# A four-layer graph network: row sums as two short-float parts, and a product moved ahead of its layer

## The chip, the cores and the metric

The kernel runs on one core of one Trainium2 chip, in one launch. The metric is the device time of one execution in microseconds. The engines are named as in the profile: PE (TensorE matmuls), PEld (its weight loads), DVE (VectorE), ACT (ScalarE), POOL (GpSimd) and SP (SyncE, which here issues most plain DMAs).

## The reference

There are N = 4096 nodes with 512 features and E = 65536 edges, sorted by destination. Each of four layers normalises the rows, applies a relu, runs a layer on the graph and adds the result to x. The second and third, layers 1 and 2, are the ones to see:

```python
# each layer: h = max(layernorm(x), 0); x = x + layer(h)
# layer 1; row, col = src, dst with a loop of every node appended
agg = segment_sum(vals[:, None] * x[col], row)          # vals = deg^-1/2[row] * deg^-1/2[col]
return relu(agg @ weight)
# layer 2
edge_feat = concatenate([x[src], x[dst], edge_attr], -1)
h = mish(edge_feat @ W1 + b1)
messages = mish(h @ W2 + b2)
agg = segment_sum(messages, dst)
u = mish(concatenate([x, agg], -1) @ W3 + b3)
y = x + u @ W4 + b4
return (y - mean(y)) * rsqrt(var(y) + eps) * gamma + beta
```

Layer 0 is an attention over the edges with eight heads, and layer 3 is a graph convolution like layer 1. All of it is computed in fp32.

## The kernel before

Nodes are held in NB = 32 blocks of P = 128, one node per partition. Edges are held in W = 512 tiles of 128, and U = 4 tiles make a group, so that there are NG = 128 groups. D is 512, KC = D/P = 4. A large SBUF tile `acc` holds one row per node and is what segment sums add into.

**Layer 1** (`sum_edges`, L865 to L913, which layer 3 uses as well). The table of rows times W already lies in DRAM (`ytab`). For each tile, POOL issues an indirect DMA (`gather`, L424) which fetches the 128 rows that its edges name; this runs four groups ahead, into six buffers. ACT makes a one-hot matrix of the edges' places in a window of nodes (Abs at L871, Relu at L876), and PE multiplies it with the gathered rows (L903), in fp32. Eight tiles share one PSUM bank; DVE then adds the bank into at most two blocks of `acc` (`add_window`, L436). Which layer runs is told by `tail` and `per`; layer 1 has `tail=0` and `per=PAIR=2`.

**Between** (L952 to L1034). As soon as a block of 128 nodes has all its edges, its next steps are issued beside the sums of later blocks: relu (L973), the sum with x1 (L975; the result goes to `x2`), mean and variance (L361), the reciprocal root through Ln and Exp with one Newton step (L982 to L989), the normalised relu (L990, L991, stored as `h2`), four transposes (L996), their copy to SBUF (L998), and two products with the halves of W1 (L1003). These are stored as `ptab` and `qtab` (L1011), so that layer 2 only has to gather and add two rows for an edge. `block` is a Python generator: each `yield` is a place where the sums go on. `follow` is called after every second tile; it begins block b when 16(b+1)+8 tiles have been issued and eight calls have passed since the last, and it steps the blocks that are under way. `the_rest` issues what is left at the end. `by_destination` (L261) prepares the lists of edges by destination beside layer 1 in the same way.

**Layer 2, messages** (L1143 to L1205). Before it, `acc` is filled with zeros, one half by DVE (L1059) and one by ACT (L1060). Then, for each group: gathers from `ptab` (L424) and adding gathers from `qtab` (L1085), the part of W1 that meets the edges' attributes (L1102), mish, transposes (L1109), the product with W2 (L413), mish, and a sum by destination. This sum already uses two short-float parts: a value is rounded to the type fp32r (L1122), the rest is a second fp32r value (L1123), and two fp32r matmuls (L1129) take the place of one fp32 matmul.

**Layer 2, end** (`layer2_ends`, L1211 to L1347). Blocks are taken in pairs (R = 2), in 16 steps. A step transposes h2 and the sums (L1277, copied at L1279), makes u transposed (64 matmuls on 128x256, L1302, with b3 added at L1304), runs mish through Sigmoid, Arctan and Sin (L1306 to L1308), multiplies with W4 (L413), adds h2 (L1320), normalises (`Norm2`, L1246 to L1270, with a root by bit tricks and Newton steps), applies gamma and x2 (L1330, L1332), stores x3, normalises once more and writes the relu scaled by `dis` (L1344) to `ztab` for layer 3. POOL adds b4 to h2 (L1293) and beta to x2 (L1314).

**Layer 3** (`Ending`, L1351 to L1420) sums by destination with the same `sum_edges`, and runs the last product and the output of each block beside these sums.

The order of instructions on PE, ACT, DVE and POOL is the order in which the program writes them (`tc.manual_schedule`). An engine works its queue in order, so one that waits holds up what is queued behind it; SP's queue of DMA issues is in order too. The table below gives the main names once more.

| name | what it is |
|---|---|
| `g`, `got` | gathered rows of a group, and the groups under way |
| `oh` | one-hot matrices of a group |
| `sum_ps` | PSUM bank of eight tiles' sums |
| `side`, `follow` | work issued between the sums |
| `ptab`, `qtab` | DRAM tables of h2 times the two halves of W1 |
| `tr`, `h_t`, `a_t`, `u_t` | transposes, and what is copied of them |

Of the kernel before, what the change touches and what calls it, by code (L numbers as in the profile page):

```python
# [34 lines left out]
def kernel(  # L35
# [225 lines left out]
    def by_destination(pool, ppool):  # L261
# [5 lines left out]
        three = pool.tile([P, 3, W], F32, name="three_d")  # L267
        for j in range(2):
            nc.vector.tensor_copy(three[:, j, :], ends[:, j, :])
            yield  # L270
        loc_i = pool.tile([P, W], I32, name="loc_i")
        nc.vector.tensor_scalar(loc_i, ends[:, 1, :], P - 1, None, op0=OP.bitwise_and)
        nc.vector.tensor_copy(three[:, 2, :], loc_i)
        yield
        for k, into in enumerate((d_src, d_dst, d_loc)):
            ps = ppool.tile([P, 4, P], F32, name="turn")
            of = three[:, k, :].rearrange("p (q j) -> p j q", j=U)
            for j in range(U):
                nc.tensor.transpose(ps[:, j, :], of[:, j, :], ident)
            yield  # L280
            yield
            nc.vector.tensor_copy(into.rearrange("p (g j) -> p j g", j=U), ps)
            yield
        node = three[:, 1, :]
        rise = pool.tile([P, W], F32, name="rise")
# [13 lines left out]
        down = pool.tile([1, NG], F32, name="down")  # L299
# [565 lines left out]
    def sum_edges(table, idx, loc, bi, half, per, beside=None, follow=None, tail=0):  # L865

        def made_one_hots(pool, minus, t0):

            oh = pool.tile([P, U, P], F32, name="oh")
# [6 lines left out]
            nc.scalar.activation(oh, oh, AF.Relu, scale=-1.0, bias=1.0)  # L876
            return oh, short

        with tc.tile_pool(name="edge", bufs=3) as ep, tc.tile_pool(name="edge_ps", bufs=4, space=PSUM) as eps, \
# [3 lines left out]
            got, ohs = {}, {}  # L883
            side = Side(*(beside(bp, bps) if beside else ()))
            for i in range(-4, NG):
                if i + 4 < NG:
                    g = got[i + 4] = ep.tile([P, U, D + tail], F32, name="g", bufs=6)
                    for j in range(U):
                        t = (i + 4) * U + j
                        gather(g[:, j, :], table, idx[:, t:t + 1])  # L890
                if 0 <= i + 1 < NG:
                    ohs[i + 1] = made_one_hots(ep, loc, (i + 1) * U)
                if i < 0:
                    continue
                g, (oh, short) = got.pop(i), ohs.pop(i)
# [6 lines left out]
                for j in range(U):  # L902
                    nc.tensor.matmul(ps[:, :D], oh[:, j, :], g[:, j, :D], start=i % per == 0 and j == 0,  # L903
                                     stop=i % per == per - 1 and j == U - 1)
                    if tail and j % 2:
                        follow(i * U + j + 1)
                    if j == U - 1 and i % per == per - 1:
                        add_window(i // per, bi, half, wide_at if tail else row_at, ps[:, :D + 3] if tail else ps)
                    if j % 2 and not tail:
                        side.step()  # L910
                        if follow:
                            follow(i * U + j + 1)
# [38 lines left out]

    class Between:  # L952
# [4 lines left out]
        def __init__(self, pool, ppool):  # L957
            self.pool, self.ppool, self.next, self.xs, self.going, self.since = pool, ppool, 0, {}, [], self.APART
            for b in range(self.AHEAD):
                self.load(b)  # L960
            self.w1_sb = load_w(pool, "w1_sb", w1[:2 * D])
            self.b1_bc = row_bc(pool, "b1_bc", b1)

        def load(self, b):
            if b < NB:
                self.xs[b] = self.pool.tile([P, D], F32, name="x_mid", bufs=self.AHEAD + 2)
                nc.sync.dma_start(self.xs[b], x1[b * P:(b + 1) * P, :])

        def block(self, b):
# [9 lines left out]
            nc.vector.tensor_scalar(st[:, 1:], st[:, 1:], EPS, None, op0=OP.add)  # L979
            root = pool.tile([P, 1], F32, name="root_mid", bufs=2)  # L980
# [14 lines left out]
            for k in range(KC):  # L995
                nc.tensor.transpose(ps[:, k, :], hn[:, k * P:(k + 1) * P], ident)  # L996
            h_t = pool.tile([P, KC, P], F32, name="ht_mid", bufs=2)
            nc.scalar.copy(h_t, ps)  # L998
            yield
            for k0, tab in ((0, ptab), (KC, qtab)):  # L1000
                ps = self.ppool.tile([P, D], F32, name="pq_ps", bufs=2)
                for k in range(KC):
                    nc.tensor.matmul(ps, h_t[:, k, :], self.w1_sb[:, k0 + k, :], start=k == 0, stop=k == KC - 1)  # L1003
                    if k < KC - 1:
                        yield
                pq = pool.tile([P, D], F32, name="pq", bufs=2)
                if k0:
                    nc.vector.tensor_add(pq, ps, self.b1_bc)
                else:
                    nc.scalar.copy(pq, ps)  # L1010
                nc.sync.dma_start(tab[rows, :], pq)  # L1011
                yield
# [6 lines left out]
        def follow(self, tiles):  # L1019

            self.since += 1
            if self.next < NB and self.since >= self.APART and tiles >= 2 * PAIR * U * (self.next + 1) + PAIR * U:
# [3 lines left out]

        def the_rest(self):
            while self.next < NB or self.going:
                if self.next < NB and (len(self.going) < 2 or not self.next % 2):
# [4 lines left out]
                self.step()  # L1034

# [9 lines left out]
    with tc.tile_pool(name="between", bufs=1) as bp, tc.tile_pool(name="between_ps", bufs=1, space=PSUM) as bps, \  # L1045
# [3 lines left out]
                  lambda pool, ppool: (by_destination(pool, ppool),), between.follow)  # L1049
# [4 lines left out]
    zero = const.tile([P, NB // 2], F32, name="zero")  # L1054
    nc.gpsimd.memset(zero, 0.0)
# [3 lines left out]
    nc.vector.memset(acc[:, :NB // 2, :D], 0.0)  # L1059
    nc.scalar.activation(acc[:, NB // 2:, :D], zero.unsqueeze(2).to_broadcast([P, NB // 2, D]), AF.Copy)  # L1060
# [561 lines left out]
```

## Time and profile before

| what | value |
|---|---|
| time, median of 3 runs | 5313.34 us (5311.9 to 5313.63) |
| the profiled execution, its own time | 5308.45 us |
| its span in the profile | 5306.7 us |
| mean granted PE clock | 0.981 |
| layer 0 and the start of layer 1 | 0 to 948 us |
| layer 1's sums, with Between | 948 to 1672 us |
| layer 2, messages | 1672 to 4234 us |
| layer 2, end | 4234 to 4616 us |
| layer 3 | 4616 to 5307 us |
| gathers of layer 1 (`g<-ytab`) | 512, mean 952 ns |
| adding gathers of layer 2 (`pg<-qtab`) | 512, mean 1718 ns |

The stages were told apart by the first and last instruction of their tiles: the first gather of layer 1 is issued at 947.94 us, the last at 1614.88, the last matmul of its sums begins before 1642.46, and the first gather of layer 2 is issued at 1672.29. In the lines of the timeline the first number is the start in microseconds from the span's begin, the second the time that the group of instructions took, then come the engine, the line of the kernel, the operation, output and inputs by their names in the program, shapes, and the number of instructions; brackets hold the idle time of the engine ahead of it and what ended that. In a table by stage the busy time of each engine stands with its count of instructions, then the granted PE clock, the mean share of the DMA engines in use, and GB/s.

### The profile page before, as it was taken

The page shows a single profiled execution, that of the slowest core. Times are in us where ns is not written, and L with a number is a line of the kernel's source. Part 1 is how long each engine was busy: PE and PEld are TensorE (multiplying, and loading weights), DVE is VectorE, ACT ScalarE, POOL GpSimd, SP SyncE. Part 2 cuts the span into 40 slices and gives each one's busy share as a digit, 9 for nine tenths or more (in the row PEclk, how much of TensorE's full clock was granted, in tenths as well). Part 3 has the DMA queues.
Part 4 walks back from the last instruction along what each step waited for, and adds up shares of the span by engine and source line. Part 5 has one row for each costly group of instructions (what it writes and reads, how often), then busy time and mean ns, then how long its engine had stood idle before and what let it go on. Part 6 is the DMA issues. An engine that isn't in the chain of part 4 may idle for free. (4 is left out here: it accounts for less than half of the span.)

```text
span 5306.7 us, 57905 instructions
## 1 busy us (share of the span) xinstructions
PE 5032.9 (95%) x17786; PEld 2790.3 (53%) x17786; DVE 3521.8 (66%) x5888; ACT 3453.1 (65%) x5301; POOL 2931.7 (55%) x2605
## 2 busy tenths in 40 slices
PE   6799999799997999999999999999999899778999
PEld 4477777344443555555555555555555577433444
DVE  8689998233333777777777777777777757633343
ACT  1267766344444888888888888888888644455554
POOL 0177775677774655555555555555555122277775
PEclk9899999899998999999999999999999999899999
DMA  3388886788885655555555555555555233377786
GB/s 109 102 237 249 251 241 192 234 265 261 265 261 149 129 111 118 114 114 112 116 115 114 113 115 115 114 112 114 117 114 112 64 89 94 120 212 221 228 250 189
DMA packets 350047, 842.90 MB, mean 159 GB/s; under 512 B 65184, under 2 KB 81568, under 8 KB 349728
## 3 DMA queue, kind: packets, MB, share of 16 engines
q0 software_dynamic: 237568, 673.87, 52.0%
q1 hardware_dynamic: 112160, 165.22, 9.4%
q8 instruction: 145, 2.38, 0.2%
q14 instruction: 174, 1.43, 0.1%
HBM read 753.67 MB, written 85.23 MB: 158 GB/s over the span
## 5 line engine op out<-in xcount | busy, mean ns | idle before, releaser
L413 PE MATMUL m_ps<-w_sb,h_t 128*128 128x512 f32 x4096 | 1821.0, 593 | 0.5 <-ACT h_t L1111 0.5
L413 PEld LDWEIGHTS m_ps<-w_sb,h_t 128*128 128x128 f32 x4096 | 758.5, 190 | 808.5 <-issue 796.9
L424 POOL DMA_INDIRECT pg<-ptab,d_src x512 | 497.1, 971 | 988.0 <-ACT h_t L1111 811.8
L903 PE MATMUL sum_ps<-g,oh 128*128 128x512 f32 x2048 | 970.4, 606 | 25.5 <-DMA w_sb<-in_L_gnn_W_dram 11.6
L1085 POOL DMA_INDIRECT pg<-qtab,d_dst x512 | 879.4, 1718 | 158.8 <-issue 144.4
L424 POOL DMA_INDIRECT rows<-htab,s_dst x512 | 492.3, 962 | 399.3 <-issue 369.8
L903 PEld LDWEIGHTS sum_ps<-g,oh 128*128 128x128 f32 x2048 | 380.0, 192 | 505.8 <-issue 424.5
L424 POOL DMA_INDIRECT g<-ytab,s_dst x512 | 487.2, 952 | 233.9 <-issue 124.2
L424 POOL DMA_INDIRECT g<-ztab,d_src x512 | 489.4, 956 | 207.1 <-issue 136.8
L1111 ACT COPY h_t<-tr_ps 128x512 f32<-128x512 f32 x512 | 275.2, 589 | 429.5 <-PE tr_ps L1109 429.3
L704 PE MATMUL sum_ps<-rows,oh 128*128 128x261 f32 x2048 | 495.2, 389 | 26.7 <-DVE rows L698 26.6
L1161 DVE TENSOR_TENSOR pg<-pg,small_ps 128x512 f32<-128x512 f32 x512 | 318.6, 683 | 188.6 <-PE small_ps L1102 150.2
L704 PEld LDWEIGHTS sum_ps<-rows,oh 128*128 128x128 f32 x2048 | 377.1, 190 | 104.2 <-DVE rows L698 37.7
L436 DVE SCALAR_TENSOR_TENSOR acc<-sum_ps,s_half,acc 128x522 f32 (+1 forms) x256 | 193.2, 755 | 336.6 <-PE sum_ps L903 301.7
L436 DVE SCALAR_TENSOR_TENSOR acc<-sum_ps,d_half,acc 128x515 f32 x256 | 193.2, 755 | 333.7 <-PE sum_ps L903 244.9
L1129 PE MATMUL small_ps<-parts,oh 128*128 128x512 f32 x1024 | 310.9, 446 | 13.4 <-DVE oh L419 13.4
L1123 DVE TENSOR_TENSOR parts<-z,parts 128x1024 fp32r<-128x1024 f32 x256 | 313.6, 1225 | 8.9
L1109 PEld LDWEIGHTS tr_ps<-ident,pg 128*128 128x128 f32 x2048 | 240.3, 141 | 146.3 <-issue 146.3
L436 DVE SCALAR_TENSOR_TENSOR acc<-small_ps,d_half,acc 128x512 f32 x256 | 192.3, 751 | 171.9 <-PE small_ps L1129 152.5
L1198 DVE TENSOR_TENSOR pg<-pg,qg 128x1024 f32<-128x1024 f32 x256 | 301.4, 1219 | 0.7 <-ACT qg L1195 0.7
L1109 PE MATMUL tr_ps<-ident,pg 128*128 128x128 f32 x2048 | 266.4, 273 | 11.4 <-DVE pg L1198 11.4
L1102 PE MATMUL small_ps<-w1e,et 64*128 64x512 f32 x1024 | 264.3, 627 | 11.4 <-DVE pg L1161 6.9
(292 smaller groups left out, 7988.2 us busy)
## 6 DMA issues: line engine op xcount, KB each, us to landing
eg<-in_edge_attr_dram SPq DMA_DIRECT2D x128, 128.0 KB, 2.8
xt<-in_x_dram SPq DMA_DIRECT2D x8, 1024.0 KB, 5.8
htab<-acc SPq DMA_DIRECT2D x32, 256.0 KB, 2.0
x_row<-in_x_dram SPq DMA_DIRECT2D x32, 256.0 KB, 4.3
rows<-htab,s_dst POOLq DMA_INDIRECT x512
x<-x_row SPq DMA_DIRECT2D x32, 256.0 KB, 3.8
ytab<-acc SPq DMA_DIRECT2D x32, 256.0 KB, 4.5
x_mid<-x SPq DMA_DIRECT2D x32, 256.0 KB, 5.2
```

Of the source, the lines that this page charges most:

```text
L413: nc.tensor.matmul(ps, h_t[:, k, :], w_sb[:, k0 + k, :], start=start and k == 0, stop=stop and k == KC - 1)
L424: nc.gpsimd.indirect_dma_start(out=dst_ap, out_offset=None, in_=table, in_offset=bass.IndirectOffsetOnAxis(ap=idx, axis=0))
L436: nc.vector.scalar_tensor_tensor(at, ps, half[:, k, i:i + 1], at, op0=OP.mult, op1=OP.add)
L704: nc.tensor.matmul(ps[:, c, :HW], oh[:, j + k, :], rows[:, j + k, c * HW:(c + 1) * HW], start=j + k == 0, stop=j + k == GT - 1)
L903: nc.tensor.matmul(ps[:, :D], oh[:, j, :], g[:, j, :D], start=i % per == 0 and j == 0, stop=i % per == per - 1 and j == U - 1)
L1085: nc.gpsimd.indirect_dma_start(out=pg[:, j, :], out_offset=None, in_=qtab, in_offset=bass.IndirectOffsetOnAxis(ap=d_dst[:, t:t + 1], axis= ...
L1109: nc.tensor.transpose(h_ps[:, k, :], h[:, j, k * P:(k + 1) * P], ident)
L1111: nc.scalar.copy(h_t, h_ps)
L1123: nc.vector.tensor_sub(parts[:, 1], m, parts[:, 0].bitcast(F32))
L1129: nc.tensor.matmul(ps, oh[:, j, :], parts[j // 2][:, k, j % 2, :], start=j == 0 and k == 0, stop=j == U - 1 and k == 1)
L1161: nc.vector.tensor_add(nxt[:, j], nxt[:, j], ps)
L1198: nc.vector.tensor_mul(h[i][:, half], h[i][:, half], qg[:, half])
```

## The change

The change has these parts.

- In layer 1 `sum_edges(split=True)` rounds the gathered rows on ACT to fp32r, two tiles at a time; DVE subtracts this from the rows and writes the rest as fp32r too (`in_two`). The one-hots are fp32r. Each tile has two fp32r matmuls in place of one fp32 matmul. Gathers run three groups ahead, into four buffers. Layer 3 keeps the old form.
- `Between` multiplies h2 with the first half of W3 as well, adds b3, and stores this as a third table, `utab`. The products of a block are issued three matmuls to two steps; a block begins six tiles later than before; it sets its own rows of `acc` to zero after having read them, and the two large fills are gone. The last two blocks' products are issued together, all of `ptab`, then of `qtab`, then of `utab`.
- In layer 2's messages, `Shifted` loads a block's rows of h2 and x2, adds b4 to one and beta to the other in one DVE instruction, and stores them back.
- The end of layer 2 loads only the second half of W3. It transposes the sums, multiplies with 512 columns at once, adds the row of `utab`, and runs mish in the natural layout; u is then transposed for the product with W4. Means come from `accum_out` of the additions, variances from Square with `accum_out` on ACT (`Spread`), and the last normalisation, relu and scale are one ACT instruction per block. POOL has no work left there.
- `by_destination` works with two tiles in place of three.

The diff, without `by_destination`, the constants and the repeated pass for unusual inputs:

```diff
-    def sum_edges(table, idx, loc, bi, half, per, beside=None, follow=None, tail=0):
+    def sum_edges(table, idx, loc, bi, half, per, beside=None, follow=None, tail=0, split=False):
...
-            oh = pool.tile([P, U, P], F32, name="oh")
+            oh = pool.tile([P, U, P], F32R if split else F32, name="oh")
+            raw = oh.bitcast(F32) if split else oh
...
-            nc.scalar.activation(oh, oh, AF.Relu, scale=-1.0, bias=1.0)
+            nc.scalar.activation(oh, raw, AF.Relu, scale=-1.0, bias=1.0)
...
+        def in_two(pool, g):
+            made = []
+            for j in range(0, U, 2):
+                parts = pool.tile([P, 2, 2, D], F32R, name="parts", bufs=3)
+                nc.scalar.copy(parts[:, 0], g[:, j:j + 2, :])
+                nc.vector.tensor_sub(parts[:, 1], g[:, j:j + 2, :], parts[:, 0].bitcast(F32))
+                made.append(parts)
+            return made
...
-            for i in range(-4, NG):
-                if i + 4 < NG:
-                    g = got[i + 4] = ep.tile([P, U, D + tail], F32, name="g", bufs=6)
+            far = 3 if split else 4
+            for i in range(-far, NG):
+                if i + far < NG:
+                    g = got[i + far] = ep.tile([P, U, D + tail], F32, name="g", bufs=4 if split else 6)
...
                 if 0 <= i + 1 < NG:
+                    if split:
+                        two[i + 1] = in_two(ep, got.pop(i + 1))
                     ohs[i + 1] = made_one_hots(ep, loc, (i + 1) * U)
...
-                    nc.tensor.matmul(ps[:, :D], oh[:, j, :], g[:, j, :D], start=i % per == 0 and j == 0,
-                                     stop=i % per == per - 1 and j == U - 1)
+                    rows = [parts[j // 2][:, k, j % 2, :] for k in range(2)] if split else [g[:, j, :D]]
+                    for k, row in enumerate(rows):
+                        nc.tensor.matmul(ps[:, :D], oh[:, j, :], row, start=i % per == 0 and j == k == 0,
+                                         stop=i % per == per - 1 and j == U - 1 and k == len(rows) - 1)
+                    if j % 2:
+                        side.step()
                         follow(i * U + j + 1)
                     if j == U - 1 and i % per == per - 1:
                         add_window(i // per, bi, half, wide_at if tail else row_at, ps[:, :D + 3] if tail else ps)
...
+            nc.vector.memset(acc[:, b, :D], 0.0)
+            yield
...
-            for k0, tab in ((0, ptab), (KC, qtab)):
...
+            if self.late is not None:
+                self.late.append((b, h_t))
+                return
+            made, ending = 0, None
+            for w in range(3):
+                going = self.product(b, h_t, w)
+                for _ in range(KC):
+                    next(going)
+                    made += 1
+                    if made % 3 != 1:
                         yield
+                        if ending:
+                            next(ending, None)
+                            ending = None
+                ending = going
+            next(ending, None)
...
-            if self.next < NB and self.since >= self.APART and tiles >= 2 * PAIR * U * (self.next + 1) + PAIR * U:
+            if self.next < NB and self.since >= self.APART and tiles >= 2 * PAIR * U * (self.next + 1) + 2 * PAIR * U - 2:
...
-    nc.vector.memset(acc[:, :NB // 2, :D], 0.0)
-    nc.scalar.activation(acc[:, NB // 2:, :D], zero.unsqueeze(2).to_broadcast([P, NB // 2, D]), AF.Copy)
+        def load(self, pool, b):
+            self.rows = pool.tile([P, 2, D], F32, name="rows_mid", bufs=1)
+            for k, tab in enumerate((h2, x2)):
+                nc.sync.dma_start(self.rows[:, k, :], tab[b * P:(b + 1) * P, :])
+        def put(self, b):
+            nc.vector.tensor_add(self.rows, self.rows, self.by)
+            for k, tab in enumerate((h2, x2)):
+                nc.sync.dma_start(tab[b * P:(b + 1) * P, :], self.rows[:, k, :])
...
+                if now(i) and i % (NG // NB) == 0:
+                    shifted.load(lp, i // (NG // NB))
+                if now(i) and i % (NG // NB) == 2:
+                    shifted.put(i // (NG // NB))
```

The new loop of the end of layer 2 (the old one is printed above):

```python
            for p in range(groups + 3):
                now = lambda k: 0 <= k < groups
                load(us, utab, "u_sb", p + 1, 3)
                load(hs, h2, "h2_sb", p, 3)
                load(xs, x2, "x2_sb", p, 4)
                if now(p - 2):
                    nc.vector.tensor_mul(u[p - 2], u[p - 2], zu.pop(p - 2))
                if now(p - 3):
                    y, norm = rows_of(p - 3), first.pop(p - 3)
                    norm.square(y)
                    norm.sharpen()
                    xt, nxt = xs[p - 3], Spread()
                    for j in range(R):
                        nc.vector.scalar_tensor_tensor(y[:, j, :], y[:, j, :], norm.minus[:, j:j + 1], gamma_bc,
                                                       op0=OP.add, op1=OP.mult)
                        nc.vector.scalar_tensor_tensor(xt[:, j, :], y[:, j, :], norm.rstd[:, j:j + 1], xt[:, j, :],
                                                       op0=OP.mult, op1=OP.add, accum_out=nxt.total[:, j:j + 1])
                    nxt.centre()
                    nc.sync.dma_start(blocks_of(x3, (p - 3) * R, R), xt)
                if now(p):
                    a_t[p] = turned("a_t", turn("tr_a", rows_of(p)))
                if now(p - 1):
                    aa, uu = a_t.pop(p - 1), us.pop(p - 1)
                    z = zu[p - 1] = lp.tile([P, R, D], F32, name="zu")
                    u_ps = multiply(0, aa, w3_sb, "u_ps")
                    nc.vector.tensor_add(z[:, 0, :], uu[:, 0, :], u_ps)
                if now(p - 2):
                    u_t = turned("u_t", turn("tr_u", u.pop(p - 2)))
                if now(p - 3):
                    nxt.square(xt)
                if now(p - 1):
                    u_ps = multiply(1, aa, w3_sb, "u_ps")
                    nc.vector.tensor_add(z[:, 1, :], uu[:, 1, :], u_ps)
                    t = u[p - 1] = lp.tile([P, R, D], F32, name="u_t_in")
                    nc.scalar.activation(t, z, AF.Sigmoid, scale=-1.0)
                    nc.scalar.activation(t, t, AF.Arctan)
                    nc.scalar.activation(t, t, AF.Sin, bias=half_pi, scale=-2.0)
                if now(p - 3):
                    nxt.sharpen()
                    ...
                    for j in range(R):
                        nc.scalar.activation(acc[:, b0 + j, :D], xt[:, j, :], AF.Relu,
                                             scale=scale[:, j:j + 1], bias=shift[:, j:j + 1])
                    nc.sync.dma_start(ztab[b0 * P:(b0 + R) * P, :D].rearrange("(b p) d -> p b d", p=P), rows_of(p - 3))
                if now(p - 2):
                    hh, y, norm = hs.pop(p - 2), rows_of(p - 2), Spread()
                    for j in range(R):
                        o_ps = multiply(j, u_t, w4_sb, "o_ps")
                        nc.vector.scalar_tensor_tensor(y[:, j, :], o_ps, 1.0, hh[:, j, :], op0=OP.mult, op1=OP.add,
                                                       accum_out=norm.total[:, j:j + 1])
                    norm.centre()
                    first[p - 2] = norm
```

## The prediction

> **What bounds the kernel now.** I read the page first (its busy shares), then the table of engines by stage, then the timeline inside the two stages that the diff touches and inside layer 2's messages, which already use the short-float form that the change brings to layer 1.
>
> ```profile
> PE 5032.9 (95%) x17786; PEld 2790.3 (53%) x17786; DVE 3521.8 (66%) x5888; ACT 3453.1 (65%) x5301; POOL 2931.7 (55%) x2605
> ```
>
> TensorE is busy 95% of the span, yet that is a mean over five stages. By stage:
>
> ```profile
> core 0: us, PE busy (x) PEld busy (x) DVE busy (x) ACT busy (x) POOL busy (x), PEclk, DMA share, GB/s
> 948.00:1672.00 724.00, 688.18 (x1684) 309.43 (x1684) 248.72 (x526) 307.97 (x792) 487.62 (x515) 0.97 0.79 247
> 1672.00:4234.00 2562.00, 2527.30 (x8452) 1303.78 (x8453) 1975.74 (x2433) 2081.34 (x1667) 1376.54 (x1024) 0.99 0.57 114
> 4234.00:4616.00 382.00, 359.41 (x1532) 269.91 (x1530) 258.78 (x699) 174.53 (x209) 84.62 (x32) 0.98 0.28 85
> ```
>
> The rows are layer 1's sums, layer 2's messages and the end of layer 2. In each PE is the fullest engine. But in layer 1 POOL has 488 of 724 us in the gathers alone (0.30 us of issue after each is not in it) and DMA is at 0.79. So a cheaper PE in layer 1 soon meets another limit. The timeline of layer 1 (start, duration, engine):
>
> ```profile
> 1301.94 0.95 POOL L424 DMA_INDIRECT g<-ytab,s_dst  x1 [0.30 <-issue]
> 1303.19 0.95 POOL L424 DMA_INDIRECT g<-ytab,s_dst  x1 [0.30 <-issue]
> ...
> 1304.12 1.88 PE L903 MATMUL sum_ps<-g,oh 128*128 128x512 f32 x4
> ...
> 1305.84 1.02 PE L1003 MATMUL pq_ps<-w_sb,ht_mid 128*128 128x512 f32 x2
> ...
> 1306.70 1.88 PE L903 MATMUL sum_ps<-g,oh 128*128 128x512 f32 x4
> ```
>
> PE repeats every 2.58 us for two row sums and one product of Between (records there count two instructions for an fp32 matmul): 0.859 each. A gather takes 0.95 + 0.30 = 1.25 us of POOL. A block of 16 tiles and 8 products is 24×0.859 + 0.44 for four transposes = 21.04 us, which is also the distance of successive transposes at L996. POOL needs 16×1.25 = 20.0 of these: it has 1.0 us of slack per block.
>
> **What the skill says.** "FP8 and Floating Point Precision", TensorE Precision Notes: a true FP32 product takes four passes, reduced precision one. The trace agrees: 0.859 us against 0.23 in layer 2, where seven weight loads that pace the short-float matmuls take 1.58 us (second line; 2500.71 to the next group of matmuls, (2502.34−2500.71)/7 = 0.233).
>
> ```profile
> 2500.31 2.41 PE L1129 MATMUL small_ps<-parts,oh 128*128 128x512 f32 x8
> 2500.71 1.58 PEld L1129 LDWEIGHTS small_ps<-parts,oh 128*128 128x128 f32 x7 [0.24 <-issue]
> ...
> 2502.34 0.41 PEld L413 LDWEIGHTS m_ps<-w_sb,h_t 128*128 128x128 f32 x2
> ...
> 2514.67 1.22 DVE L1123 TENSOR_TENSOR parts<-z,parts 128x1024 fp32r<-128x1024 f32 x1
> ```
>
> "SBUF — State Buffer", Who interferes with whom: VectorE and GpSimd share a port pair as an exclusive lock, taken by a VectorE operation with two SBUF inputs. The trace agrees. The 0.68 us addition of two SBUF tiles holds a gather to its own end plus about 0.1:
>
> ```profile
> 4835.51 0.68 DVE L1389 TENSOR_TENSOR x_end<-x_end,t_end 128x512 f32<-128x512 f32 x1
> 4835.63 1.38 POOL L424 DMA_INDIRECT g<-ztab,d_src  x1 [0.30 <-issue]
> ...
> 4837.32 0.95 POOL L424 DMA_INDIRECT g<-ztab,d_src  x1 [0.30 <-issue]
> ```
>
> The same holds for L1191 and L1198 in layer 2: 121 and 124 gathers that start under them take 1.81 and 1.96 against 1.54 us. Operations with a PSUM input (L436, L1008) and tensor_scalar (L990, L991) delay none, though the page's section on the two sides names 2-port modes too; the measurement decides. "ScalarE activation tables: per-element evaluation and per-set limits", What a function is on this engine: changing the set costs a load of 1283 ns. The trace has 1.28 at L1306, twice per group of the end of layer 2; the change keeps both.
>
> **The change part by part.** (1) *Layer 1's PE.* A tile becomes two matmuls of 0.23 = 0.46, saving 0.40; 512 tiles save 204 us. The third product adds 4×0.859 per block, 110 us over 32. A block's PE: 16×0.46 + 12×0.859 + 0.44 = 18.1 us, 2.9 less.
>
> (2) *ACT and DVE of layer 1.* From the window 1100:1580 (some 23 blocks) a block has 9.4 us on ACT, 7.1 on DVE. Added are eight fp32r copies 128x1024 on ACT, 1.06 each (L1306's Sigmoid on 128x1024 in SBUF is the nearest row), making 17.9; on DVE eight subtractions like L1123, 1.22 each, one bias addition 0.69 and the memset of a row, 0.43: about 18.0. Both fit in 20 us, barely. Queued behind each ACT copy, which waits for two gathers, are the one-hots of the same group and Between's ACT steps; PE waits for these. From the end of a group's first half on PE to the next group's one-hots that chain is 1.06+1.28+0.63 plus handovers, 3.2, against some 3.5 us of PE work between: no bound alone, no slack either.
>
> (3) *The subtractions and the gathers.* This is the disputed cost. L884's subtraction has two SBUF inputs and lasts 1.22 us; a gather starts every 1.25. At a random phase it holds the next start for (1.10²/2)/1.25 = 0.48 us on average. Two per group: 5.0+0.96, less what lies in pauses, so I take 5.9 us per group. Bounds: 5.0 if the phase always misses, 7.2 if each costs its full 1.1. A gain below 5.0 is excluded, as POOL's own 4×1.25 stays. Block: 23.6 against 21.04.
>
> (4) *DMA.* A block moves 262 GB/s × 21.04 us = 5.5 MB now (window 1100:1580); a third store of 0.26 MB makes it 5.77, and at 20 us the share of 0.84 there would become 0.84×1.05×1.05 = 0.93. It is not the bound at 23.6.
>
> (5) *Tail of layer 1.* Now the last tile's matmul comes at 1642.5, the last transposes at 1657.0, the first gather of layer 2 at 1672.3. After: the gathers run 948 + 127×5.9 + 4.7 = 1702, and from the last one to the last tile 4.5 (median from gather start to landing) + 1.06 + 1.22 + queues, 9.5: 1711.5. From there to the transposes 14.5 − 6.2 (the fills L1059/L1060, 6.9 and 7.0 us, that DVE work stands behind now) + 4.3 (five products of block 29 still to run) = 12.6; then 24 products of 0.859, 20.6; then store and landing as now, 3.5. First gather at 1748: **+76 us**. With 5.0 it would be 1635, −37. Every 0.1 us of group period is 12.8 us.
>
> (6) *Loads and steps moved.* w3's first half (1 MB), b3, b4 and beta go to earlier places, on SP's queue, under layer 1's ramp (first gathers there take 6.5 us instead of 4.5): +2. by_destination with two tiles has the same work: 0. The gate of a block moves by six tiles: inside the tail above.
>
> (7) *Shifted in layer 2.* Per four iterations two loads and two stores of 256 KB on SP, at a DMA share of 0.57, and one DVE addition of 1.22. DVE has pauses of 0.17 and 1.24 us ahead of L1155 and L1161; PE, with 2527 of 2562 us busy, sets the time. It costs nothing while the addition lies in those pauses. It also has two SBUF inputs and may delay one gather by 1.1, while POOL is busy 54%. Without cover: 32×1.22 = 39. I take +2.
>
> (8) *End of layer 2.* Sixteen steps (pairs of blocks). Now:
>
> ```profile
> 4403.50 1.28 ACT L1306 ACT_TABLE_LOAD   x1
> ...
> 4409.31 1.32 ACT L1344 ACTIVATE acc<-h,scales 128x512 f32<-128x512 f32 x2
> 4409.68 1.04 PE L1277 MATMUL tr<-ident,h_sb 128*128 128x128 f32 x8
> ...
> 4432.11 1.04 PE L1277 MATMUL tr<-ident,h_sb 128*128 128x128 f32 x8
> ```
>
> A step is 22.43 us, all PE: 16 transposes, 64 matmuls of 0.216 (13.8) and 8 of 0.859 (6.9). After: 16 transposes 1.75 and 16×0.859 = 15.5. Then ACT and DVE are late next, as each waits for the other: two Squares 1.6, 13 small DVE operations 2.4 (4422.91 to 4425.32 now), four scalar_tensor_tensor 3.0, centre 0.2, two Squares 1.6, table to Sin 5.8 (the first and second lines), two Relus 1.5 and handovers: 16.5. I take 16.5. Stage: first Square at 28, 14 steps more, 27 of drain, the last step in it: 286 against 381 (4234.7 to 4615.8), **−94**; at 15.5 us it is −109, at 18 −74. POOL's additions (3.1 and 2.4 us) that block DVE there now vanish.
>
> Sum: +76 + 2 + 2 − 94 = −14 on the profiled execution of 5308.45 (span 5306.7): 5294. It lies 4.9 below the median of the runs, 5313.34, so 5299 in those terms.
>
> **The rivals.** *B, the collisions stay few*: a subtraction comes at a phase fixed by the landing of its gathers, and may fall while POOL is mid-gather; layer 1 is then bound by POOL at 5.0 to 5.3. For it: POOL's records are regular (0.30 pauses). Against: landings vary from 3.7 to 6.3 us. Time at 5.15: 5299 − 0.75×128 = 5203 (5184 to 5222). *C, slower*: gathers, copies, subtractions and one-hots lock into a loop, since every late gather makes its copy and the one-hots behind it late, and PE with 18 of 20 us cannot catch up. In place: L883/L884. Price at 6.25 us per group: +45, 5344 (to 5370 at 6.45). It decides from 6.1 us per group on, where the loss in layer 1 exceeds the 94 us of the end. *D, the end or Shifted disappoint*: addition exposed, 5338; or layer 2's end stays at 18 us, 5319.
>
> **How the numbers follow.** Forecast A (5.5 to 6.1 us, 5265 to 5325): 0.52. B 0.22, C 0.23, D 0.03. What the measurement can tell from no change is 0.2%, 5303 to 5324. Of A 0.34 lies below it and 0.17 within, 0.01 above; B is faster, C slower, D slower: faster 0.56, same 0.17, slower 0.27. The range reaches into B and C: 5195 to 5345.
>
> **What would show it.** Right: layer 1's gathers with a mean near 1.15 to 1.2 us instead of 0.95, the long ones under the subtraction; blocks 23.6 us apart; PE idle in layer 1, waiting for parts; layer 2's messages unchanged at about 2562 us; steps of 16.5 us at its end with ACT the fullest. Wrong: gathers at 0.95 and blocks of 20 to 21 us (B); blocks over 24.4 (C); PE still back to back at the end.

## The result, and the profile after

The changed kernel takes 5277.35 us (median of 4 runs, 5270.05 to 5277.63) against 5313.49 us before (5311.9 to 5313.76): a ratio of 0.9929, with a 95% interval from 0.9912 to 0.9947. The forecast was 5299. The medians differ by 36 us; the profiled executions differ by 31 us of span, 5275.7 against 5306.7, as the one before ran some 5 us faster than its median. All that follows compares these two executions, unless another chip is named.

First the page's busy shares after the change:

```profile
PE 4892.3 (93%) x17274; PEld 2704.6 (51%) x17274; DVE 3796.9 (72%) x6239; ACT 3716.9 (70%) x5620; POOL 2956.6 (56%) x2572
```

PE lost 141 us of work (5032.9 before), and the profiled execution became 31 us shorter. The table by stage shows where the two part; the rows are again layer 1's sums, layer 2's messages and the end of layer 2.

```profile
core 0: us, PE busy (x) PEld busy (x) DVE busy (x) ACT busy (x) POOL busy (x), PEclk, DMA share, GB/s
951.00:1734.00 783.00, 646.14 (x1940) 364.29 (x1940) 563.98 (x845) 553.75 (x1057) 573.94 (x516) 0.93 0.78 241
1734.00:4272.00 2538.00, 2515.21 (x8425) 1297.80 (x8426) 1997.69 (x2447) 2072.56 (x1662) 1401.04 (x1024) 0.99 0.61 127
4272.00:4588.00 316.00, 267.05 (x790) 132.27 (x789) 196.50 (x716) 209.32 (x289) 0.00 (x0) 0.92 0.46 143
```

In layer 1 PE fell from 688 to 646 us of work, and yet the stage grew from 724 to 783. PE is no longer what sets it. DVE's work more than doubled (249 to 564), and POOL's busy time rose from 488 to 574 us, though it issues the same 512 gathers. The end of layer 2 is shorter, and PE is the fullest engine there.

The exact places of the stages come from the first and last start of tiles (the two numbers before the last semicolon). First before, then after:

```profile
L424 POOL DMA_INDIRECT g<-ytab,s_dst x512: 940/946/1467, 947.9 to 1614.9; - x171
L424 POOL DMA_INDIRECT pg<-ptab,d_src x512: 940/962/1961, 1672.3 to 4130.2; - x171
L424 POOL DMA_INDIRECT g<-ztab,d_src x512: 942/946/1457, 4620.5 to 5264.6; - x171
L413 PE MATMUL m_ps<-w_sb,h_t x4096: 589/592/697, 1712.0 to 4211.9; 128*128 128x512 f32 x196
```

```profile
L422 POOL DMA_INDIRECT g<-ytab,s_dst x512: 942/946/2002, 951.4 to 1684.0; - x171
L422 POOL DMA_INDIRECT pg<-ptab,d_src x512: 942/967/1963, 1734.0 to 4192.1; - x171
L422 POOL DMA_INDIRECT g<-ztab,d_src x512: 942/946/1437, 4588.2 to 5231.7; - x171
L411 PE MATMUL m_ps<-w_sb,h_t x4096: 590/593/697, 1773.0 to 4273.8; 128*128 128x512 f32 x196
```

| from, to | before, us | after, us | difference |
|---|---|---|---|
| start, to the first gather of layer 1 | 947.9 | 951.4 | +3.5 |
| to the first gather of layer 2 | 724.4 | 782.6 | +58.2 |
| to the last product with W2 | 2539.6 | 2539.8 | +0.2 |
| to the first gather of layer 3 | 408.6 | 314.4 | −94.2 |
| to the end | 686.2 | 687.5 | +1.3 |

They sum to −31.0. So the end of layer 2 gives 94 us, and layer 1 takes 58 of them back.

Why layer 1 does so is seen in its groups of instructions on the page (busy time and mean ns of one, then idle time before them and what ended it). First the gathers before, then the groups after:

```profile
L424 POOL DMA_INDIRECT g<-ytab,s_dst x512 | 487.2, 952 | 233.9 <-issue 124.2
```

```profile
L422 POOL DMA_INDIRECT g<-ytab,s_dst x512 | 573.5, 1120 | 210.4 <-issue 138.6
L917 PE MATMUL sum_ps<-parts,oh 128*128 128x512 f32 x1024 | 366.6, 480 | 110.2 <-ACT oh L875 97.6
L883 ACT CAST parts<-g 128x1024 fp32r<-128x1024 f32 x256 | 267.2, 1044 | 183.0 <-DMA g<-ytab,s_dst 122.5
L884 DVE TENSOR_TENSOR parts<-g,parts 128x1024 fp32r<-128x1024 f32 x256 | 307.2, 1220 | 114.4 <-ACT parts L883 113.8
```

Read them as a chain. PE waits for the one-hots (97.6 us). ACT, which makes them, waits for gathered rows at the copy that is queued ahead of them (122.5). And the gathers have nothing to wait for but their own issue (138.6): POOL issues without a break, but one gather takes 1120 ns where it took 952. The account closes: from the first gather to the last it is 732.6 us; the gathers fill some 573 of these and the pauses of 0.30 us after each another 156, so that hardly 4 us are left in which POOL waited for anything else. (Before, the same count leaves 25 us of other waits in 667.0.) The timeline shows which gathers are long:

```profile
1304.67 0.95 POOL L422 DMA_INDIRECT g<-ytab,s_dst  x1 [0.30 <-issue]
1305.92 1.87 POOL L422 DMA_INDIRECT g<-ytab,s_dst  x1 [0.30 <-DMA g<-ytab,s_dst]
1308.09 0.95 POOL L422 DMA_INDIRECT g<-ytab,s_dst  x1 [0.30 <-issue]
...
1305.75 1.23 DVE L884 TENSOR_TENSOR parts<-g,parts 128x1024 fp32r<-128x1024 f32 x1 [3.46 <-ACT parts L883]
1306.89 0.69 DVE L992 TENSOR_TENSOR pq<-pq_ps,b_bc 128x512 f32<-128x512 f32 x1
...
1308.53 1.22 DVE L884 TENSOR_TENSOR parts<-g,parts 128x1024 fp32r<-128x1024 f32 x1 [0.95 <-ACT parts L883]
```

The second gather starts at 1305.92, 0.17 us into a subtraction that ends at 1306.98. It lasts 1.87 us, 0.92 more than the other two. The one at 1308.09 starts when no subtraction is under way; the next subtraction begins at 1308.53, while this gather runs, and doesn't lengthen it. Of the 512 gathers 196 start under a subtraction, with 0.60 us of it left on average, and these take 1.40 us, 0.45 more than the rest; those that start under the bias addition, which has one input from PSUM (L992, 32 of them), take 0.95. So a gather is delayed by what is left of the subtraction, less some 0.15 us.

### The profile page after: what moved, and what is told of

Its sections match the earlier page's. It is cut to its first block, busy times and chain, and to the rows that moved or that the text cites. A ratio compares the mean times of both kernels' runs of the same rounds, so it can differ in the third digit from the quotient of the medians.

```text
span 5275.7 us, 58505 instructions
## 1 busy us (share of the span) xinstructions
PE 4892.3 (93%) x17274; PEld 2704.6 (51%) x17274; DVE 3796.9 (72%) x6239; ACT 3716.9 (70%) x5620; POOL 2956.6 (56%) x2572
## 5 line engine op out<-in xcount | busy, mean ns | idle before, releaser
L1144 POOL DMA_INDIRECT pg<-qtab,d_dst x512 | 903.7, 1765 | 158.7 <-issue 151.7
L422 POOL DMA_INDIRECT g<-ytab,s_dst x512 | 573.5, 1120 | 210.4 <-issue 138.6
L917 PE MATMUL sum_ps<-g,oh 128*128 128x512 f32 x1024 | 482.9, 612 | 0.0
L917 PE MATMUL sum_ps<-parts,oh 128*128 128x512 f32 x1024 | 366.6, 480 | 110.2 <-ACT oh L875 97.6
L883 ACT CAST parts<-g 128x1024 fp32r<-128x1024 f32 x256 | 267.2, 1044 | 183.0 <-DMA g<-ytab,s_dst 122.5
L884 DVE TENSOR_TENSOR parts<-g,parts 128x1024 fp32r<-128x1024 f32 x256 | 307.2, 1220 | 114.4 <-ACT parts L883 113.8
L917 PEld LDWEIGHTS sum_ps<-parts,oh 128*128 128x128 f32 x1024 | 194.5, 199 | 266.2 <-ACT oh L875 164.1
L917 PEld LDWEIGHTS sum_ps<-g,oh 128*128 128x128 f32 x1024 | 187.1, 193 | 243.4 <-issue 210.6
```

What stands on the lines that cost most here:

```text
L422: nc.gpsimd.indirect_dma_start(out=dst_ap, out_offset=None, in_=table, in_offset=bass.IndirectOffsetOnAxis(ap=idx, axis=0))
L883: nc.scalar.copy(parts[:, 0], g[:, j:j + 2, :])
L884: nc.vector.tensor_sub(parts[:, 1], g[:, j:j + 2, :], parts[:, 0].bitcast(F32))
L917: nc.tensor.matmul(ps[:, :D], oh[:, j, :], row, start=i % per == 0 and j == k == 0, stop=i % per == per - 1 and j == U - 1 and k == len(ro ...
L1144: nc.gpsimd.indirect_dma_start(out=pg[:, j, :], out_offset=None, in_=qtab, in_offset=bass.IndirectOffsetOnAxis(ap=d_dst[:, t:t + 1], axis= ...
```

## The experiments

The runs of the first five parts are set against the changed kernel's 5277.35 us, except where another chip is named: on the chips on which they ran the kernel before takes 5310.96 and 5312.1 us, within 3 us of the 5313.49 above.

**The port alone.** The subtraction gives way to scalings with one SBUF input. The result is then not the reference's any more.

```diff
-                nc.vector.tensor_sub(parts[:, 1], g[:, j:j + 2, :], parts[:, 0].bitcast(F32))
+                for k in range(2):
+                    nc.vector.tensor_scalar(parts[:, 1, k, :], g[:, j + k, :], s_half[:, 0, 0:1], s_half[:, 0, 0:1],
+                                            op0=OP.mult, op1=OP.mult)
```

> The changed kernel with the subtraction of two SBUF tiles replaced by two scalings of 128x512 with one SBUF tile as input (about 1.1 us together, against 1.22), so that the second part isn't the rest any more; everything else, the copies and the matmuls too, stays. Port theory: the subtraction holds the gathers' port, which costs layer 1 0.69 us per group over 4 x 1.25; without it the gathers' mean goes from 1.12 back to 0.95 us, a group takes 5.0 to 5.1 instead of 5.73, and the kernel 5277 - 128 x 0.65 = about 5194. Rival, a loop of queues: copies, one-hots and matmuls wait for each other on ACT, DVE and PE; DVE's busy time is nearly unchanged, so the group stays at 5.6 to 5.7 and the time at 5265 to 5277.

Measured: 5209.0 us (ratio to the kernel before 0.9807, 0.979 to 0.9823). In its page:

```profile
L422 POOL DMA_INDIRECT g<-ytab,s_dst x512 | 506.1, 989 | 210.8 <-issue 126.4
L885 DVE TENSOR_SCALAR parts<-g,s_half 128x512 fp32r<-128x512 f32 x512 | 257.2, 555 | 70.4 <-DMA g<-ytab,s_dst 34.7
```

The copies and all matmuls are there, DVE has 257 of its 307 us, and still 68 us are gone. This run alone doesn't refute a loop of queues, since the scalings do not wait for ACT's copy as the subtraction does, and so the loop is shorter too. POOL's account does: here as in the changed kernel gathers and pauses fill the stage (505 and 156 of 665.9 us), and what fell is the length of the gathers. A group takes (1614.2−948.3)/127.75 = 5.21 us, not 5.0 to 5.1: a gather that starts under these scalings lasts 1.03 us, so they are not quite free, and 15 that start under an addition of two SBUF tiles in Between (L1005) last 1.24.

**The same work in halves.**

```diff
+                for k in range(2):
+                    nc.vector.tensor_sub(parts[:, 1, k, :], g[:, j + k, :], parts[:, 0, k, :].bitcast(F32))
```

> The changed kernel with each subtraction of 128x1024 issued as two of 128x512 (0.69 us each); same result. Port theory: an operation of length L holds a gather that starts at a random point in it, with a mean delay that goes with the square of L - 0.12; (0.57^2)/(1.10^2) = 0.27, and twice as many operations, so 0.54 of the delay: 0.69 becomes 0.37 us per group, 128 x 0.32 = 41 us less, about 5236. Rival, DVE or the chain of queues as the bound: DVE gets 8 x 0.16 = 1.3 us more per block, so the time stays or rises to 5277 to 5310.

Measured: 5230.75 us (0.985, 0.9834 to 0.9867), against 5236 expected.

```profile
L422 POOL DMA_INDIRECT g<-ytab,s_dst x512 | 523.4, 1022 | 210.7 <-issue 131.5
L885 DVE TENSOR_TENSOR parts<-g,parts 128x512 fp32r<-128x512 f32 x512 | 324.8, 690 | 60.5 <-ACT parts L883 60.3
```

DVE does more (325 against 307 us), and the kernel is 46 us faster: DVE's load was not the limit, the length of one instruction was. With the quarters below, whose times overlap with its own, it is the fastest kernel here that computes all of the reference.

**Quarters.**

> The changed kernel with each subtraction of 128x1024 issued as four of 128x256 (about 0.4 us each); same result. The halves (128x512) gave 5231 and 5.35 us per group, where the whole gave 5.73. Port theory by the square law: (0.28^2) x 4 / (1.10^2) = 0.26 of 0.69, 0.18 us, so 5.18 to 5.2 per group: about 5210. Rival: eight instructions per group more on DVE cost as much as they save, 5225 to 5260.

This first try ran on a chip on which the kernel before takes 5693.68 us: 5689.71 against it, no difference (0.9976 to 1.0006). On that chip layers 0 and 3 were longer too, which have no subtractions, so it is no test of the law. It shows something else. Against whole subtractions on the same chip (the run without the pass, below) the 512 gathers became shorter, from 552 to 516 us in all, but POOL's other waits between them rose from some 77 to 186 us, and layer 1 took 916 us instead of 839. There the quarters cost time; why POOL waits longer stays open.

> The subtraction as four of 128x256 once more. On a chip where the kernel before takes 5311 us: by the square law 5.18 to 5.2 us per group and 5210 us; by the rival, more instructions on DVE cost as much as they save, 5225 to 5260. On a chip where it takes 5676 or more: 5690, as in the first try, which tells nothing on the law, because layers 0 and 3 show that something other than the port holds the gathers there.

Measured: 5234.03 us (0.9856, 0.9839 to 0.9872), no better than halves: 5.36 us per group, where the law had 5.18 to 5.2. The gathers on the page, then a stretch of the timeline:

```profile
L422 POOL DMA_INDIRECT g<-ytab,s_dst x512 | 522.1, 1020 | 210.7 <-issue 123.1
```

```profile
1283.76 2.77 DVE L886 TENSOR_TENSOR parts<-g,parts 128x256 fp32r<-128x256 f32 x8
1284.61 2.73 POOL L422 DMA_INDIRECT g<-ytab,s_dst  x1 [0.30 <-DMA g<-ytab,s_dst]
```

The eight instructions of 0.418 us follow each other in 2.77 us, 0.336 apart, so each begins before the one ahead has ended. The gather at 1284.61 waits through all that are left. Five gathers lasted over 2.3 us in this way; in the halves none was over 1.47. They cost some 8 us of the 22 by which the law missed. Another 5 come from 23 gathers that now start under the addition of two SBUF tiles in Between (L1006) and last 1.18; the law left that addition out. Most quarters follow each other as closely as these eight, so why only five gathers were held through a whole run stays open.

**Only the split undone.**

```diff
-                  lambda pool, ppool: (by_destination(pool, ppool),), between.follow, split=True)
+                  lambda pool, ppool: (by_destination(pool, ppool),), between.follow)
```

> The changed kernel with layer 1's sums in fp32 as before (no copies, no subtractions, gathers four groups ahead), all else of the change kept. PE then has 28 x 0.859 + 0.44 = 24.5 us per block against 22.9 measured now, so that layer 1 should take 32 x 1.6 = 51 us more: about 5328, gathers back to 0.95 us. Rival: the split costs as much through its collisions as it saves, and the time lies at 5277 or below.

Measured: 5327.24 us (1.0031, 1.002 to 1.0043). The stages without the split gain and lose as before, but layer 1 takes 833.6 us from first gather to the first of layer 2, 51.0 more than the changed kernel.

```profile
L422 POOL DMA_INDIRECT g<-ytab,s_dst x512 | 485.6, 948 | 330.7 <-PE sum_ps L917 153.6
```

The gathers are back at 948 ns and now wait for PE (153.6), which is busy all of the 480 us from 1100 to 1580. So with the third product in layer 1 the split is worth 50 us, collisions and all; without the split the change would have been a loss of 16 us.

**Only the third product left out.**

```diff
+                if w < 2:
                     nc.tensor.matmul(ps, h_t[:, k, :], w_sb[:, k0 + k, :], start=k == 0, stop=k == KC - 1)
```

> The changed kernel with the four matmuls of the third product left out (its table gets a constant in place of the product; the copy, the store and the wait for it stay as a DVE operation with one SBUF input of about 0.55 us). Port theory: layer 1 is bound by gathers that the subtractions hold up, PE has 4.8 us to spare per block, so only the tail is shorter, by 8 x 0.859 = 7 us: about 5270. Rival, PE still matters in layer 1: up to 32 x 3.4 = 110 us less, 5170 to 5230.

Measured: 5262.87 us (0.9911, 0.9894 to 0.9928). Of 110 us of PE work taken away, 14 arrive in the time: PE's time in layer 1 was covered. PE's busy time in the stage (here 948 to 1718 us) fell by 57 us only, from 646 to 589, at a granted clock of 0.83 instead of 0.93.

```profile
L422 POOL DMA_INDIRECT g<-ytab,s_dst x512 | 566.6, 1107 | 210.5 <-issue 140.1
```

The gathers are still held. First to last gather it is 724.5 us instead of 732.6, and the way from the last to layer 2 is 45.2 us instead of 50.0.

**The pass for b4 and beta, and the roots.** Both ran on the chip where the kernel before takes 5694 us; they concern stages that there take as long as elsewhere, and are compared with each other.

```diff
-                if now(i) and i % (NG // NB) == 0:
-                    shifted.load(lp, i // (NG // NB))
-                if now(i) and i % (NG // NB) == 2:
-                    shifted.put(i // (NG // NB))
```

> The changed kernel without the pass in layer 2's messages that adds b4 and beta to the rows of h2 and x2 (its 64 loads, 64 stores and 32 additions are left out; b4 and beta are zero in these inputs). The prediction put this pass at 2 us, as DVE's pauses and POOL's slack cover it: about 5276, and the first to the last product with W2 stays at 2500 us. Rival: the addition is exposed, or delays gathers that PE waits for: up to 39 us less, 5238.

```diff
-                    for _ in range(3):
+                    for _ in range(1):
                         nc.vector.tensor_mul(half, self.rstd, self.rstd)
```

> The changed kernel with one Newton step in place of three in the roots of the end of layer 2 (12 small DVE operations fewer per pair of blocks; the roots are less exact). The prediction had ACT and DVE waiting for each other as the bound there, 16.2 us per step as measured. Of the 12 operations six lie between the squares and the scalings, 1.2 us; the loop would be 15.0 and PE with 15.5 the bound: 15 x 0.6 = 9 us less, about 5268. Rival: PE, or something else, already sets the step: 5277, no change.

Measured: 5633.45 us without the pass, 5620.71 with it and with one Newton step. From the first to the last product with W2 it is 2500.5 us without the pass and 2500.8 with it: it costs nothing that can be seen. From the last such product to layer 3's first gather it is 314.7 us with three Newton steps and 301.4 with one, 13 us less. The start of a pair's transposes on PE, first in the changed kernel, then with one Newton step:

```profile
4405.39 1.04 PE L1338 MATMUL tr_a<-ident,acc 128*128 128x128 f32 x8
...
4421.38 1.04 PE L1338 MATMUL tr_a<-ident,acc 128*128 128x128 f32 x8
...
4437.57 1.04 PE L1338 MATMUL tr_a<-ident,acc 128*128 128x128 f32 x8
```

```profile
4668.75 1.04 PE L1338 MATMUL tr_a<-ident,acc 128*128 128x128 f32 x8
4684.24 1.04 PE L1338 MATMUL tr_a<-ident,acc 128*128 128x128 f32 x8
```

15.99 and 16.19 us apart in the one, 15.49 in the other. In the changed kernel the first full steps are 15.48 too, PE's own work; from the middle of the stage on they are 16.19, and the run without the pass, on the same chip as the one with one Newton step, has both in the same order. With one Newton step all full steps are 15.48 or 15.49. So the loop of ACT and DVE is shown as the bound of the later steps: it is longer than PE's step by 0.7 us. That PE has a lead which takes some steps to use up fits this, but was not tested apart.

**A table that is split where it is written.** Two forms; the second moves the DVE instruction.

```diff
+                    self.two = ep.tile([P, 2, D], F16, name="row_two")
+                    nc.scalar.activation(self.two[:, 0, :], self.ps, AF.Copy, scale=by)
                     nc.scalar.activation(self.row, self.ps, AF.Copy, scale=by)
+                    nc.vector.scalar_tensor_tensor(self.two[:, 1, :], self.ps, by, self.two[:, 0, :],
+                                                   op0=OP.mult, op1=OP.subtract)
```

> A version that keeps the two parts and takes the subtraction out of layer 1: the rows of the table are stored as two fp16 parts (the rounded value and the rest, 4 bytes per element as before), made where the table is written at the end of layer 0: one more ACT instruction and one DVE instruction with a PSUM input per block of 128 nodes. Layer 1 gathers them four groups ahead and multiplies both parts with fp16 one-hots; no copies and no subtractions there. Port theory: gathers at 0.95 us, POOL bound, 5.0 to 5.1 per group: 128 x 0.68 = 87 us less, a shorter way from the last gather to the last matmul, another 3, and 0 to 20 us more in layer 0: 5187 to 5210. Rival: with 0.26 MB more per block than the kernel before and 20 us per block, DMA becomes the bound and the group stays above 5.4: 5235 or more.

> The changed kernel itself once more, on the same chip as the next two, since the last four runs were on a chip on which the kernel before takes 5694 instead of 5311 us. On a chip where the kernel before takes 5311: 5270 to 5278. On one where it takes 5694: as the run without the pass for b4 and beta, 5633, if that pass costs nothing.

> The table in two fp16 parts, as before, but the DVE instruction that makes the second part is issued at the end of the group instead of right behind ACT's first part: the first form made layer 0 some 48 us longer. On a chip where the kernel before takes 5311 us: port theory, gathers at 0.95 us and 5.0 to 5.1 us per group in layer 1, 87 us less there, 0 to 20 more in layer 0: 5187 to 5210. Rival, DMA as the bound in place of the port: 5.4 us and more per group, 5235 and up; and if the wait wasn't what layer 0 lost by, another 48.

> The changed kernel with each subtraction issued as two of 128x512 and with two Newton steps in place of three at the end of layer 2 (roots less exact). On a chip where the kernel before takes 5311 us: 5231 from the halves, less 9 to 13 at the end of layer 2, since one step less takes 0.58 us from the loop and PE with 15.5 us is then the bound: 5220. Rival: the loop wasn't the bound and the one step saves nothing: 5231.

All four fell on chips where the kernel before is slow (5694 us for the first, 5676 for the other three). Measured: 5642.74, 5638.24, 5651.28 and 5649.66 us. The ratio of the changed kernel to the one before is the same there, 0.9921 (0.989 to 0.9953). The gathers of layer 1 in the changed kernel, then with the table in parts, on that chip:

```profile
L422 POOL DMA_INDIRECT g<-ytab,s_dst x512: 940/946/1972, 1151.0 to 1934.0; - x171
```

```profile
L423 POOL DMA_INDIRECT g<-ytab,s_dst x512: 940/947/1403, 1204.9 to 1945.2; - x171
```

A group takes (1934.0−1151.0)/127.75 = 6.13 us in the first and 5.79 in the second, which is about the rate of layer 3's gathers on this chip, 5.73, where nothing was changed. So without subtractions layer 1 falls to what this chip gives elsewhere, but that is far from 5.0. Layer 0 became 54 us longer (1204.9 against 1151.0), and moving the instruction did not help (48 in the first form, against its neighbours): what layer 0 loses by stays open, as does what this table would give on the first chip. The halves brought nothing there either. Layer 1 took 17 us more with them: the 512 gathers took 527 us in place of 556, but POOL's other waits rose from some 73 to 120. With two Newton steps, in the same run, the end of layer 2 took 306.0 us against 315.9, and its full steps were 15.48 us.

## Why the prediction was right, by its steps

The forecast was a gain of 14 us; 36 were measured, well inside the range of 5195 to 5345 but more than twice as much. The mechanism was right, and one term of the sum, the collisions, was too large.

**What bounds the kernel.** Right. The order of limits in layer 1 is POOL's gathers, held by the subtractions, then PE; leaving out the third product and leaving out the second SBUF input show it from both sides. The price of a matmul on parts was right too: they follow each other at 0.235 us (median), 0.23 in the working.

**Step 3, the collisions.** The mechanism was right, the size was too large. Predicted: 0.48 us per subtraction. Measured: the gathers took 573.5−487.2 = 86 us more, 0.34 for each of 256 subtractions; 77% of them hold a gather where the sum had 88%, each for 0.45 us where it had 0.55. A group took (1684.0−951.4)/127.75 = 5.73 us, not 5.9, which is 21 us from the first gather to the last. In spans the forecast missed by 17, −14 against −31.0: these 21, less what the tail and the start took back. The other 5 of the 22 by which the time was overestimated are the distance of the profiled execution before from its median, which the forecast added. The words "to its own end plus about 0.1" have a wrong sign; the sum took 1.10 of 1.22 us, less 0.12, and that is near what the gathers show. Why fewer collide than at a random phase wasn't tried.

**Steps 1, 2 and 4.** Blocks came 4×5.73 = 22.9 us apart. PE was not the bound, nor was DMA with a share of 0.83 from 1100 to 1580. PE had more to do than the 18.1 us per block of the working: it was busy for 417 of these 480 us, which is 19.9 us per block. The chain of copies and one-hots was not the bound either, as POOL's account shows.

**Step 5, the tail.** From the last gather to the first of layer 2 it took 50.0 us; the working had 46.2.

**Step 6.** Predicted +2. The first gather of layer 1 came 3.5 us later, but in the runs of the same code on other chips with a fast kernel before it came at 947.0 to 948.5 us, where it was 947.9 before. So the 3.5 are scatter, and no cost of the moved loads is seen there.

**Step 7.** 0.2 us for the pass, predicted 2; shown by leaving it out.

**Step 8.** −94.2 us against −94. That this fits so well is luck in part. Two of its parts were off and cancelled: the steps took 15.48 and then 16.19 us instead of 16.5 throughout, and the stage's two ends took the rest. (28 + 14×16.5 + 27 is also 95 less than 381, not 94.) The claim that ACT would be the fullest engine there was wrong: PE has 267 of 316 us, ACT 209, DVE 196. Here a loop bound the later steps with no engine full.

**Rivals.** B (collisions stay few) would have been 5203; taking the port away gives 5209, so its price was right and its premise wrong. C decided from 6.1 us per group on; that wasn't reached on this chip. On the slower one the changed kernel took 6.13, and was still faster than the kernel before it.

## What to carry to other kernels

When a matmul becomes cheaper by work on DVE, look at what POOL does at that time: here a DVE instruction with two SBUF inputs held the gathers that started under it nearly to its end (0.45 us more with 0.60 us of it left), and since POOL issued gathers without a break, this set the stage. Cutting such an instruction in two cost DVE 6% more time and gave back 46 us; cutting it in four gave no more. On the chips where the kernel before takes 5676 us and more neither helped, and layer 1 became longer. Moving work into a stage with another limit is cheap only up to that limit: the third product's 110 us of PE work cost 14 in layer 1 and were part of what made the end of layer 2 94 us shorter (the other changes there weren't tried apart), but without the split the sum is a loss.

## What the runs showed of the hardware

Chips differ in what stages with gathers take. On two of them the kernel before took 5694 and 5676 us instead of 5311; layer 2's messages, bound by PE, took the same 2500 us from the first to the last product, while layer 3 took 5.73 us for four gathers instead of 5.04. The gathers themselves were no slower: layer 3's 512 took POOL 486 us there and 489 on the first chip. The difference is in stops of mostly 2.5 to 3.2 us, three or four groups apart, in which POOL waits. What they come from stays open. A gain that rests on gathers has to be measured on more than one chip.

Short DVE instructions that follow each other closely can hold a gather as one long one does: 2.73 us for one gather under a run of eight. This was rare, 5 gathers of 512.

POOL can hold DVE as well. At the end of layer 2 in the kernel before, under POOL's addition of beta, a DVE operation on 128x2 took 2.28 us, 14 times, where it takes 0.17 elsewhere. The changed kernel has no POOL work there.

```profile
4413.88 2.35 POOL L1314 TENSOR_TENSOR xs<-xs,beta_bc 128x1024 f32<-128x1024 f32 x1
4413.98 2.28 DVE L1257 TENSOR_SCALAR down<-st 128x2 f32<-128x2 f32 x1
```
